# Adding the last expert blocks to the tokens by one-hot products instead of by scatter

## The chip, the cores and the metric

The kernel runs on one core of one Trainium2 chip. A core has engines that run side by side, each with its own instruction queue: TensorE (PE, matrix products; its weight loads are shown as PEld), VectorE (DVE), ScalarE (ACT), GpSimd (POOL) and SyncE (SP). They meet through semaphores. Sixteen DMA engines move data between the chip's DRAM and SBUF, the on-chip memory of 128 partitions; transfers are issued from the queues of SP, ACT and POOL. Products land in PSUM, from which DVE or ACT takes them. The metric is the device time of one execution in microseconds (us).

## The reference

Two layers over 625 tokens of width 768, with graph edges. Each layer adds a graph network and a linear attention to the tokens, and then a mixture of eight experts of which each token takes two:

```python
xn = _layernorm(x)
x = x + _L0_gnn_ref(xn, ...) + _L0_mix_ref(xn, ...)
x = x + _L0_ffn_ref(_layernorm(x), ...)     # 8 experts, top 2, three matrices each
xn = _layernorm(x)
x = x + _L1_gnn_ref(xn, ...) + _L1_mix_ref(xn, ...)   # graph attention
x = x + _L1_ffn_ref(_layernorm(x), ...)     # 8 experts, top 2, two matrices each
return x
# an expert mixture:
for e in range(8):
    h = gelu(x @ W1[e] + b1[e]); ...; y = h @ W_last[e] + b_last[e]
    out = out + gate[:, e:e+1] * y
```

All of it is f32. Biases and scales are random, so none of it can be left out.

## The kernel before

Tokens are kept in five blocks of T = 125. The experts work on gathered rows: a token's two places among its experts' rows are computed on chip (class Dispatch), and full blocks of 128 slots and half blocks of 64 slots are formed, each with one expert. Block numbers below NPB = 13 are full, those from 13 on half. RUN lists the 13 blocks that always run, in order; it ends in 8, 15, 9. MORE lists those which run only if the routing needs them; they stand in a conditional on the value `used` (L1330 in layer 0, L1681 in layer 1), which is not entered with these inputs.

A block gathers its token rows from DRAM by an indirect DMA on POOL (`gather`, L532), multiplies through the expert's matrices, scales by the gate into a tile `y` and adds `y` to the token rows of `sums_d[layer]`, in DRAM, by an indirect DMA with addition, again on POOL (`scatter_add`, L536). Two scatters into the same table go one after the other. `sums_d` was filled before with the tokens and the gated last biases. Layer 0's blocks are interleaved by hand (`blocks0`: six stages a block, a new block every three steps); a half block packs its two halves of columns into the two halves of the partitions, so its y has 128 rows of 384 and is added to half rows of the table. Layer 1's blocks (`block1`) load their weights on SP through shared buffers.

The order of instructions on each engine is found by a scheduler at build time, from the program's order and a model of times; dependencies are tracked by tile and region. In a conditional, nothing moves in or out.

Around layer 0's end: a tile `msum` with the counts of edges between tokens is loaded on ACT's queue (L1323), and behind the conditional 25 transposes (L1338) and 5 copies (L1339) make `mult` of it, used by the graph attention (`weights_of`, L1390 and L1410). Then layer 1 begins: for each token block, `sums_d[0]` is read (L367, on SP), normalised (L243 to L232), transposed (L187), multiplied by `L1_gnn_W1` (L201, 512 columns, 12 products of two instructions each) into `xl`, normalised again and transposed into `hT`. `sums_d[0]` is read once more much later, as the residual.

At the kernel's end, behind the second conditional, `sums_d[1]` is copied to the output in DRAM by two DMAs (L1683, L1685).

A few names: `ps_tile` gives one of four PSUM tiles of two banks; `token_rows` moves one block between DRAM and SBUF in two DMAs of 112 and 13 rows; `by_token` views a table as token blocks; `slabs` loads weights through five buffers of `wpool`.

Of the kernel before, what the change touches and what calls it, by code (L numbers as in the profile page):

```python
# [35 lines left out]
RUN = (0, 1, 2, 13, 3, 4, 5, 14, 6, 7, 8, 15, 9)  # L36
MORE = (10, 11, 12, 16, 17, 18, 19, 20)
# [6 lines left out]
def kernel(ctx: ExitStack, tc: tile.TileContext, a: dict, out: bass.AP):  # L44
# [83 lines left out]
    def blk(b):  # L128
        return slice(b * T, (b + 1) * T)
# [405 lines left out]
    def scatter_add(table_d, src, rows):  # L535
        nc.gpsimd.indirect_dma_start(out=table_d, out_offset=bass.IndirectOffsetOnAxis(ap=rows, axis=0),  # L536
                                     in_=src, in_offset=None, compute_op=OP.add)

# [651 lines left out]

    later = ctx.enter_context(ExitStack())
    multp = later.enter_context(tc.tile_pool(name="multp", bufs=1))
    mult = multp.tile([T, NB, N], F32, name="mult")


    with tc.tile_pool(name="msums", bufs=1) as msums:
        msum = msums.tile([128, NB, DQ * 128], F32, name="msum")
        with tc.tile_pool(name="work0", bufs=2) as moe:
            places_of = Dispatch(moe, moe, router)
            idx, es_i, used = places_of.idx, places_of.es_i, places_of.used  # L1200
            router.weigh()
            in_order.close()
            router.add_biases(x, moe)
            token_rows(by_token(sums_d[0]), x, True)
            es_hot, gate = places_of.gates()
            c1 = expert_biases(moe, moe, es_hot, columns_of["fb1"].rearrange("p (e c) -> p e c", e=8), 2, "c1")
            c2 = expert_biases(moe, moe, es_hot, columns_of["fb2"].rearrange("p (e c) -> p e c", e=8), 3, "c2")
            def hidden(a_, n, width, bias, name):

                ps = ps_tile()  # L1210
                for c in range(n):
                    nc.tensor.transpose(ps[:width, 0, c * 128 : (c + 1) * 128], a_[:, c * width : (c + 1) * width], ident)
                h_ = moe.tile([128, 3, 128], F32, name=name, bufs=3)
                for c in range(n):
                    nc.scalar.activation(h_[:width, c, :], ps[:width, 0, c * 128 : (c + 1) * 128], AF.Gelu,
                                         bias=bias[:, c : c + 1])
                return h_

            gates = []

            def block0(b, spare_pool=None):

                ex = nc.sync.value_load(es_i[0:1, b : b + 1], min_val=0, max_val=7)
                w12 = moe.tile([128, 1920], F32, name="w12", bufs=3)
                w1 = w12[:, :1152].rearrange("p (k o) -> p k o", k=KC)
                w2 = w12[:96, 1152:1920].rearrange("p (k o) -> p k o", k=2)
                nc.sync.dma_start(w1, expert(a["L0_ffn_W1"], ex).rearrange("(k p) o -> p k o", p=128))
                nc.sync.dma_start(w2, expert(a["L0_ffn_W2"], ex).rearrange("(k p) o -> p k o", p=96))
                w3 = (spare_pool.tile([128, 2304], F32, name="w3", bufs=1) if spare_pool else
                      wpool.tile([128, 2304], F32, name="w"))  # L1230
                w3 = w3.rearrange("p (k o) -> p k o", k=3)
                nc.sync.dma_start(w3, expert(a["L0_ffn_W3"], ex).rearrange("(k p) o -> p k o", p=128))
                if b >= NPB:
                    yield from block0_half(b, w1, w2, w3)
                    return
                xg = moe.tile([128, D], F32, name="xg", bufs=4)
                gather(xg, tokens_d[0], idx[:, b : b + 1])
                xT = moe.tile([128, KC, 128], F32, name="xT", bufs=3)
                evac(xT, to_slot_columns(xg, KC), b)
                yield  # L1240
                ps = ps_tile()
                for k in range(KC):
                    nc.tensor.matmul(ps[:, 0, :192], xT[:, k, :], w1[:, k, :], start=(k == 0), stop=(k == KC - 1))
                a1 = moe.tile([128, 192], F32, name="a1")
                nc.vector.tensor_copy(a1, ps[:, 0, :192])
                yield
                h1 = hidden(a1, 2, 96, c1[:, b, :], "h1")
                yield
                ps = ps_tile()
                for k in range(2):  # L1250
                    nc.tensor.matmul(ps[:, 0, :384], h1[:96, k, :], w2[:, k, :], start=(k == 0), stop=(k == 1))
                a2 = moe.tile([128, 384], F32, name="a2")
                nc.vector.tensor_copy(a2, ps[:, 0, :384])
                yield
                h2 = hidden(a2, 3, 128, c2[:, b, :], "h2")
                yield
                y = moe.tile([128, D], F32, name="y")
                ps = ps_tile()
                for h in range(2):
                    for k in range(3):  # L1260
                        nc.tensor.matmul(ps[:, h, :384], h2[:, k, :], w3[:, k, h * 384 : (h + 1) * 384],
                                         start=(k == 0), stop=(k == 2))
                if not gates:
                    gates.extend(gate())
                nc.vector.tensor_scalar(halves(y), ps[:, :, :384], gates[0][:, b : b + 1], None, op0=OP.mult)
                scatter_add(sums_d[0], y, idx[:, b : b + 1])

            def block0_half(b, w1, w2, w3):

                i = b - NPB  # L1270
                xg = moe.tile([128, D], F32, name="xg", bufs=4)[:64]
                gather(xg, tokens_d[0], idx[:64, b : b + 1])
                xT = moe.tile([128, KC, 128], F32, name="xT", bufs=3)[:, :, :64]
                evac(xT, half_slot_columns(xg), b)
                yield
                ps = ps_tile()
                for k in range(KC):
                    for j, p in enumerate(sides):
                        nc.tensor.matmul(ps[p, 0, :96], xT[:, k, :], w1[:, k, j * 96 : (j + 1) * 96],
                                         start=(k == 0), stop=(k == KC - 1))  # L1280
                a1 = moe.tile([128, 192], F32, name="a1")
                nc.vector.tensor_copy(a1[:, :96], ps[:, 0, :96])
                yield
                ps = ps_tile()
                nc.tensor.transpose(ps[:96, 0, :128], a1[:, :96], ident)
                h1 = moe.tile([128, 3, 128], F32, name="h1", bufs=3)
                for c in range(2):
                    nc.scalar.activation(h1[:96, c, :64], ps[:96, 0, c * 64 : (c + 1) * 64], AF.Gelu,
                                         bias=c1[:, b, c : c + 1])
                yield  # L1290
                ps = ps_tile()
                for k in range(2):
                    for p, c in zip(sides, (slice(0, 256), slice(256, 384))):
                        nc.tensor.matmul(ps[p, 0, : c.stop - c.start], h1[:96, k, :64], w2[:, k, c],
                                         start=(k == 0), stop=(k == 1))
                a2 = moe.tile([128, 384], F32, name="a2")
                nc.vector.tensor_copy(a2[:, :128], ps[:, 0, :128])
                nc.vector.tensor_copy(a2[:64, 128:256], ps[:64, 0, 128:256])
                yield
                ps = ps_tile()  # L1300
                nc.tensor.transpose(ps[:, 0, :128], a2[:, :128], ident)
                nc.tensor.transpose(ps[:, 0, 128:192], a2[:64, 128:256], ident[:64, :64])
                h2 = moe.tile([128, 3, 128], F32, name="h2", bufs=3)
                for c, at in ((0, 0), (2, 64), (1, 128)):
                    nc.scalar.activation(h2[:, c, :64], ps[:, 0, at : at + 64], AF.Gelu, bias=c2[:, b, c : c + 1])
                yield
                y = moe.tile([128, D], F32, name="y")[:, :384]
                ps = ps_tile()
                for k in range(3):
                    for j, p in enumerate(sides):  # L1310
                        nc.tensor.matmul(ps[p, 0, :384], h2[:, k, :64], w3[:, k, j * 384 : (j + 1) * 384],
                                         start=(k == 0), stop=(k == 2))
# [407 lines left out]
```

## Time and profile before

| what | us |
|---|---|
| median of three runs (2404.85 to 2409.11) | 2408.49 |
| the profiled execution's own time | 2404.86 |
| its span | 2403.1 |
| PE busy | 2227.3 (93%) |
| DVE busy | 932.2 (39%) |
| ACT busy | 278.0 (12%) |
| POOL busy | 467.1 (19%) |
| scatters L536: 26, mean | 1.58 each to issue |

Times in the profile count from the start of the span. Busy times are of the profiled execution alone. The slice rows cut the span into 40 equal parts, with each engine's busy tenths; a slice is 60 us, so what happens within 20 us needs the timeline, which lists instructions by start, duration, engine and line, like ones merged ("x12"), with the engine's idle time before them and what ended it. A DMA's row there is its issue, not its transfer. An engine's sequencer (PEq, SPq and so on) has rows for semaphores and branches, given by source line.

### The profile page before, as it was taken

The numbers are of one execution on the slowest core, as the hardware profiler recorded it, in microseconds if no ns is written. First come the engines' busy times: TensorE is split into PE (matmuls) and PEld (weight loads), VectorE is DVE, ScalarE is ACT, GpSimd is POOL, SyncE is SP. The second block draws the span as 40 slices with busy tenths as digits, with TensorE's granted clock in tenths as the row PEclk, the third lists the DMA queues.
The fourth block names the chain that finished last, engine by engine and source line by source line (L and its number), as shares of the span: only waits on it lengthen the run. The fifth ranks groups of instructions, "written<-read, shape, count | busy, mean of one in ns | idle before, by whom it ended". The sixth has DMA issues, their size and how long they took to land. (4 is left out here: it accounts for less than half of the span.)

```text
span 2403.1 us, 25088 instructions
## 1 busy us (share of the span) xinstructions
PE 2227.3 (93%) x10262; PEld 1473.7 (61%) x10262; DVE 932.2 (39%) x1930; ACT 278.0 (12%) x579; POOL 467.1 (19%) x261
## 2 busy tenths in 40 slices
PE   7999989999999999999999697799999998799996
PEld 4666556777776567777776454355776555455553
DVE  7554143444443333343352521623764534411110
ACT  2111000000001100000000122212552101011110
POOL 1676633232220022222210021000000200101100
PEclk9999999999999999999999799899999999799998
DMA  9435395444432051111101699112003200779785
GB/s 352 99 53 54 66 258 149 121 124 130 130 80 78 6 191 59 64 59 53 34 1 52 218 303 271 33 73 72 1 1 131 73 13 19 287 261 391 289 337 187
DMA packets 152834, 310.82 MB, mean 129 GB/s; under 512 B 49070, under 2 KB 70706, under 8 KB 152672
## 3 DMA queue, kind: packets, MB, share of 16 engines
q1 hardware_dynamic: 91154, 232.46, 27.6%
q0 software_dynamic: 52192, 49.28, 10.6%
q10 hardware_dynamic: 9358, 27.30, 3.4%
q8 instruction: 87, 1.43, 0.3%
q14 instruction: 43, 0.35, 0.0%
HBM read 249.09 MB, written 63.58 MB: 130 GB/s over the span
## 5 line engine op out<-in xcount | busy, mean ns | idle before, releaser
L912 PE MATMUL ps<-cnt,parts 125*128 125x314 bf16 x2880 | 392.3, 299 | 12.7 <-DVEq L1098 8.5
L912 PEld LDWEIGHTS <-parts 125*128 125x128 bf16 x2880 | 283.2, 98 | 121.4 <-issue 16.1
L668 POOL DMA_INDIRECT table<-val,idx x80 | 161.1, 2014 | 133.2 <-DMA table<-val,idx 58.6
L934 POOL TENSOR_TENSOR features<-w 128x1152 f32<-128x1152 f32 x14 | 37.3, 2666 | 521.7 <-issue 348.0
L960 PE MATMUL ps<-pair,w 128*128 128x314 f32 x504 | 136.8, 429 | 2.1 <-ACT pair L177 2.1
L1613 PE MATMUL ps<-w,xT 128*128 128x384 f32 x360 | 126.3, 502 | 11.3 <-DVE xT L175 6.7
L532 POOL DMA_INDIRECT xg<-tokens,d_idx x26 | 27.5, 1057 | 483.0 <-DVE gates L338 151.9
L960 PEld LDWEIGHTS ps<-pair,w 128*128 128x128 f32 x504 | 95.8, 190 | 40.4 <-ACT pair L177 2.6
L1626 PE MATMUL ps<-w,hT 128*128 128x384 f32 x360 | 119.2, 487 | 0.0
L201 PE MATMUL ps<-w,hT 128*125 128x384 f32 x360 | 117.8, 486 | 0.0
L1613 PEld LDWEIGHTS ps<-w,xT 128*128 128x128 f32 x360 | 68.0, 196 | 56.0 <-DVE xT L175 8.1
L177 ACT COPY features<-ps 128x628 f32<-128x628 f32 (+1 forms) x15 | 10.5, 703 | 766.2 <-PE ps L912 765.3
L201 PEld LDWEIGHTS ps<-w,hT 128*125 128x125 f32 x360 | 67.1, 188 | 46.9
L1626 PEld LDWEIGHTS ps<-w,hT 128*128 128x128 f32 x360 | 67.5, 190 | 45.0 <-issue 0.3
L1425 PE MATMUL ps<-xl,pT 125*125 125x256 f32 (+1 forms) x300 | 81.1, 427 | 12.4 <-ACT pT L177 8.8
L536 POOL DMA_INDIRECT sums<-y,d_idx x26 | 41.1, 1581 | 220.1 <-DVE y L1630 77.3
L881 PE MATMUL ps<-w,features 128*125 128x384 f32 x240 | 82.9, 504 | 0.0
L966 DVE TENSOR_TENSOR pair<-ps,pair 128x628 f32<-128x628 f32 (+1 forms) x60 | 44.8, 746 | 97.5 <-PE ps L960 97.5
L201 PE MATMUL ps<-w,features 128*125 128x384 f32 x240 | 80.0, 493 | 0.0
L1537 POOL TENSOR_TENSOR row<-row 128x768 f32<-128x768 f32 x1 | 1.8, 1813 | 395.9 <-DVE top L1395 395.9
L210 PE MATMUL ps<-features,w 128*128 128x313 f32 x288 | 77.4, 427 | 0.0
L1425 PEld LDWEIGHTS ps<-xl,pT 125*125 125x125 f32 x300 | 56.2, 191 | 34.1 <-ACT pT L177 10.3
(423 smaller groups left out, 3355.6 us busy)
## 6 DMA issues: line engine op xcount, KB each, us to landing
w<-in_L_ffn_w_dram SPq DMA_DIRECT2D x78, 1152.0 KB
w<-in_L_gnn_W_dram SPq DMA_DIRECT2D x34, 1152.0 KB
w<-in_L_ffn_W_dram SPq DMA_DIRECT2D x13, 1152.0 KB
table<-zero SPq DMA_DIRECT2D x32, 400.0 KB
cnt<-table POOLq DMA_DIRECT2D x16, 800.0 KB
edges<-cnt POOLq DMA_DIRECT2D x8, 1600.0 KB
w<-in_L_ffn_W_dram SPq DMA_DIRECT2D x13, 576.0 KB
w<-in_L_mix_W_qkv_dram SPq DMA_DIRECT2D x6, 1152.0 KB
```

Of the source, the lines that this page charges most:

```text
L201: nc.tensor.matmul(ps[:T, h, :width], xT[:, k, blk(b)], w_of(k)[:, h * width : (h + 1) * width], start=(k == 0), stop=(k == nk - 1))
L210: nc.tensor.matmul(ps[:width, h, :NH], w_of(k)[:, c0 : c0 + width], xT[:, k, h * NH : (h + 1) * NH], start=(k == 0), stop=(k == nk - 1))
L536: nc.gpsimd.indirect_dma_start(out=table_d, out_offset=bass.IndirectOffsetOnAxis(ap=rows, axis=0), in_=src, in_offset=None, compute_op=OP.add)
L668: scatter = nc.gpsimd.indirect_dma_start(out=table_of(g, j), out_offset=bass.IndirectOffsetOnAxis(ap=idx[:, j : j + 1], axis=0), in_=val[: ...
L881: nc.tensor.matmul(ps[:T, h, :384], aggs[:, k, blk(b)], w_of(k)[:, h * 384 : (h + 1) * 384], start=(k == 0), stop=(k == KC - 1))
L912: nc.tensor.matmul(ps[:, h, :HC], parts[:, b, i, k * 128 : (k + 1) * 128], cnt[:T, b, h * HC : (h + 1) * HC], start=(b == 0 and i == 0), s ...
L934: nc.gpsimd.tensor_add(wmix[:, 1], b11, b12)
L960: nc.tensor.matmul(ps[:, j, :HC], right[:, k, c : c + 128], left(k), start=(k == 0), stop=(k == K2 - 1))
L966: nc.vector.tensor_add(total, ps[:, :n, :HC], total)
L1425: nc.tensor.matmul(o, pT[:, j, :], xl[:, j, cols], start=(j == 0), stop=(j == NB - 1))
L1613: nc.tensor.matmul(ps[:, 0, :384], xT[:, k, :], w1_of(k)[:, q * 384 : (q + 1) * 384], start=(k == 0), stop=(k == KC - 1))
L1626: nc.tensor.matmul(ps[:, h, :384], hT[:, k, :], w2_of(k)[:, h * 384 : (h + 1) * 384], start=(k == 0), stop=(k == 8))
```

## The change

Blocks 15 and 9 (LAST) of layer 0, and block 9 of layer 1, are no longer scattered before the next stage. For each a 0/1 matrix `hot` (slots by 625 tokens) is made at dispatch, by comparing the slot's token number with a row of numbers. Once y is there, PE multiplies `hot` by y for each token block and half of the columns, and DVE adds the product to the token rows, which have been read back from `sums_d` without those blocks. A new class does it:

```diff
+    class Direct:
+        def __init__(self, pool, places, name):
...
+            nc.gpsimd.iota(self.number, pattern=[[1, N]], base=0, channel_multiplier=0, ...)
+        def slots(self, b):
...
+            nc.vector.tensor_scalar(self.hot[b], self.number, at, None, op0=OP.is_equal)
+            self.y[b] = self.pool.tile([128, D if b < NPB else 384], F32, name=f"{self.name}_y{b}", bufs=1)
+        def add(self, x, t, h):
+            ps = ps_tile()
+            out_ = ps[:T, h, :384]
+            bs = sorted(self.hot)
+            for b in bs:
+                p, c = (slice(0, 128), slice(h * 384, (h + 1) * 384)) if b < NPB else (slice(h * 64, (h + 1) * 64), slice(0, 384))
+                nc.tensor.matmul(out_, self.hot[b][p, blk(t)], self.y[b][p, c], start=(b == bs[0]), stop=(b == bs[-1]))
+            c = slice(h * 384, (h + 1) * 384)
+            nc.vector.tensor_add(x[:, t, c], out_, x[:, t, c])
```

In layer 0 the reads go on ACT's queue, six DMAs into the place of `xl` (now allocated before the experts), once before the conditional and once more at the end of its body. Behind the conditional stand the two scatters, for the later read of the sums, and the ten adds. `msum` is loaded only then, into the place of a later tile, and its transposes are done in layer 1's loop over token blocks, after the second transposes of each. The loop no longer reads DRAM. A full block of LAST scales its y in two halves.

```diff
-                    if step == 12 and spare_pool is None:
-                        nc.scalar.dma_start(msum, edges_d.rearrange("b p c -> p b c"))
...
+        def tokens_again():
+            for ts in ((0, 1), (1, 3), (3, NB)):
+                for p in (slice(0, 112), slice(112, T)):
+                    nc.scalar.dma_start(x1[p, ts[0] : ts[1], :], by_token(sums_d[0])[p, ts[0] : ts[1], :])
...
         blocks0(RUN)
+        tokens_again()
         w1_of = slabs(a["L1_gnn_W1"], 1024, 2)
         with tc.If(nc.values_load(used, min_val=0, max_val=2) > 0):
             blocks0(MORE, moe)
+            tokens_again()
+        for b in LAST:
+            if b < NPB:
+                scatter_add(sums_d[0], direct.y[b], idx[:, b : b + 1])
+            else:
+                scatter_add(half_rows(sums_d[0]), direct.y[b], places_of.idx2[:, b - NPB : b - NPB + 1])
         for b in range(NB):
-            ps = ps_tile()
-            sl = slots(ps, T)
-            for j in range(NB):
-                nc.tensor.transpose(sl[:, j, :], msum[:T, j, blk(b)], ident[:T, :T])
-            nc.scalar.copy(mult[:, b, :].rearrange("p (j c) -> p j c", c=T), sl)
+            for h in range(2):
+                direct.add(x1, b, h)
...
+        msum = lay.tile([128, 8 * NP], F32, name="gT")[:, : NB * DQ * 128].rearrange("p (b c) -> p b c", b=NB)
+        nc.scalar.dma_start(msum, edges_d.rearrange("b p c -> p b c"))
...
         for b in range(NB):
             xb = part.tile([T, 1, D], F32, name="part", bufs=3)
-            token_rows(by_token(sums_d[0])[:, b, :], xb[:, 0, :], False)
-            layernorm(xb, xb, D, [0])
+            layernorm(x1, xb, D, [b], [0])
             block_to_columns(xb, xnT, KC, b, 0)
...
+            multiplicities(b)
```

In layer 1 the sums are read on SP into `x` after the blocks of RUN, and the adds and the stores of the output follow before the conditional; its body repeats both. The copy from DRAM to DRAM is gone.

```diff
+            direct = Direct(keep, places_of, "end")
+            direct.slots(RUN[-1])
...
+            def tokens_again():
+                for b in range(NB):
+                    token_rows(by_token(sums_d[1])[:, b, :], x[:, b, :], False)
+            def finish():
+                for b in range(NB):
+                    for h in range(2):
+                        direct.add(x, b, h)
+                    token_rows(out[b * T : (b + 1) * T, :], x[:, b, :], True)
             blocks1(RUN)
+            tokens_again()
+            finish()
             with tc.If(nc.values_load(used, min_val=0, max_val=2) > 0):
                 blocks1(MORE)
-        nc.sync.dma_start(out[0:624, :].rearrange("(p r) d -> p (r d)", p=48), ...)
-        nc.sync.dma_start(out[624:N, :], sums_d[1][624:N, :])
+                tokens_again()
+                finish()
```

## The prediction

> **What bounds the kernel now.** The slice rows of the page come first: TensorE (PE) is busy in 93% of the span, and few slices fall below 9 tenths. The change touches two of them: the turn from layer 0's experts to layer 1 (about 1480 to 1515 us) and the last 20 us. The chain of waits ends with the last scatter (L536) and holds nothing of the copy to the output behind it, so I read the timeline. Columns: start, duration (us), engine, line, operation, in brackets the idle time before it.
>
> ```profile
> 2384.58 0.81 PE L1626 MATMUL ps<-w,hT 128*128 128x384 f32 x2
> 2385.43 1.02 DVE L1630 TENSOR_SCALAR y<-ps,d_gate 128x768 f32<-128x768 f32 x1 [11.38 <-PE ps L1626]
> 2386.72 1.55 POOL L536 DMA_INDIRECT sums<-y,d_idx  x1 [21.23 <-DVEq L1681]
> 2393.77 0.62 SPq L1683 DMA_DIRECT2D out_dram<-sums  x1
> 2394.76 0.50 SPq L1685 DMA_DIRECT2D out_dram<-sums  x1
> ```
>
> Nothing computes after 2386.5. The last 16.7 us are scatter (to 2392.7), then the 1.9 MB copy from DRAM to DRAM, issued at 2393.77; the rows of the kernel's last line have SP draining from 2402.2 and the end at 2403.1. The timeline of the turn:
>
> ```profile
> 1483.61 1.55 POOL L536 DMA_INDIRECT sums<-y,d_idx  x1 [7.65 <-issue]
> ...
> 1485.57 6.55 PE L1261 MATMUL ps<-w,h 128*128 128x384 f32 x12 [0.52 <-ACT h L1215]
> ...
> 1490.67 1.55 POOL L536 DMA_INDIRECT sums<-y,d_idx  x1 [5.51 <-DMA sums<-y,d_idx]
> ...
> 1494.17 2.96 PE L1338 MATMUL ps<-ident,msum 125*125 125x125 f32 x25 [2.05 <-DVEq L1330]
> ...
> 1496.50 1.57 POOL L536 DMA_INDIRECT sums<-y,d_idx  x1 [4.28 <-DMA sums<-y,d_idx]
> ...
> 1503.81 36.82 SPq L367 DMA_DIRECT2D part<-sums  x10
> ...
> 1507.57 1.02 DVE L243 BATCH_NORM_STATS2 ln_st<-part 125x6 f32<-125x384 f32 x2 [2.92 <-DMA part<-sums]
> ...
> 1513.50 12.67 PE L201 MATMUL ps<-w,x 128*125 128x512 f32 x24 [1.09 <-ACT x L177]
> ...
> 1528.64 10.56 PE L201 MATMUL ps<-w,x 128*125 128x512 f32 x24 [1.18 <-DVE x L175]
> ```
>
> The three scatters are those of blocks 8, 15 and 9. Each waits for the one before; the read of the sums waits for the third, and PE has no layer-1 matmul until 1513.50. The idle time is not empty: PE spends 2.96 us of it on the transposes of the edge counts, which nothing else needs yet.
>
> What the conditional costs is in the rows of its own line:
>
> ```profile
> L1330 SPq EVENT_SEMAPHORE  x9: 17/17/17, 1493.0 to 1500.0; - x9
> ```
>
> The branch isn't taken, but SP sits in it until its loads in flight have landed (7 us). An engine whose DMAs also occur in the untaken body waits so.
>
> **The end.** Removed: the last scatter and the copy, that is, everything after 2386.5. Added: 10 products (5 token blocks, 2 halves), 10 adds, 10 stores. A 128-row, 384-column f32 product is two instructions; 6 of them took 4.03 us (L1261 at 1459.01), 0.67 each. The scaling of y's first half (0.62, row of L1661) fits under the second half's matmuls, so the products start at 2385.5 and PE ends them at 2385.5 + 10 x 0.67 = 2392.2. An add is half of L359's 0.96 (768 wide), 0.5, so VectorE (DVE) keeps up with PE; its last one ends at 2392.9. The stores of blocks 0 to 3 go out meanwhile (375 KB per 1.34 us, 280 GB/s; the DMA rows show 348 to 422 at their best). The last store: the nearest row is the read of one block, issued 1503.81 and used at 1507.57, 3.76 us. So 2396.7. With 0.3 us for leaving the branch and the 1.0 us of closing that followed the last landing before, 2398.0: **5.1 us less**. The Trainium skill ("DMA: Bandwidth & Descriptors", Anatomy of one DMA) gives about 2.0 us fixed plus bytes over 436 GB/s: 2.9 us here, 6.3 for the copy that took some 8.3 in this trace. By it the end would come 0.9 us earlier; the page's figure is for another path and too low for the copy, so I take the row.
>
> The reads that this needs: 10 DMAs on SP, issued once block 15's scatter (2363.93) has landed. SP has nothing behind its weights (last issue 2357.8); the DMA engines are 1.03 to 1.07 busy until 2372 and at 0.02 from 2375 to 2386. 1.9 MB at 300 GB/s from 2373 ends at about 2380, hidden by 5 us; past 2386 each us would show in the end.
>
> **The turn.** Removed from the path: scatters 15 and 9, and the read behind them. Scatter 8 has landed by 1490.67. The six reads now go on the ACT queue (0.38 us an issue, row of L1323), with the weight load that SP issues at 1492.2 (1.15 MB) beside them: 3.07 MB at 348 GB/s are 8.8 us from 1492.3, 1501; with the reads served first, 1498. I take 1500. ACT can leave the branch only when all six have landed (the SP row above), so splitting them by block gives nothing. Queued behind this wait on ACT: the count load, the square roots, the copies of the transposed tokens.
>
> PE now has 20 products: 13.4 us. Four PSUM buffers let 8 of them run before 1500; the other 12 follow as DVE frees buffers, 8.1 us, so 1508.5; I say 1509 for part of it at half clock. If block 0's layernorm (3.3 us on DVE) slips between the adds, as the scheduler mixed L1372 of one block among L243 of the next, the transposes follow at 1509 and L201 some 2.3 us later: 1511.3 against 1513.50. It finds a warm PE: 10.56 instead of 12.67. Gain 2.2 + 2.1 = 4.3. For the warmth, the rule ("TensorE: Matmul & The Clock Gate", HAM clock gate) says that the clock halves after about 3.4 us idle and returns after as much work. The trace is harsher: granted clock 0.50 from 1484 to 1490 after gaps of 1.3 us. By the rule a PE that stood from 1496 to 1500 costs a further 2 us, by the row less idling is enough; this speaks against the change, and is why 1509 and not 1508.5, and its 2 us are in the range.
>
> Given back: the 25 transposes of the counts (2.96) now stand after each block's second transposes in a loop in which PE is busy for 11 to 12.5 of each 13.5 us. They go ahead of the next block's transposes, so they fill no gap, and their ACT copies (0.7) precede an ACT evacuation that PE awaits: 3.0 (0 if the scheduler puts them in the gaps of 1.1 to 2.3 us, 5 with the copies). The turn: -4.3 + 3.0 = **-1.3**.
>
> **Costed at nothing.** Block 15's scaling no longer waits 4.28 us for a y buffer; PE gains at least 0.6, but the reads end later anyway. The one-hots: two compares of 128x625 (0.48, row of L1390) and small casts, 1.5 us of DVE in 2.48 idle before L1245 at 1368; 0.7 in layer 1, in 3.17 idle before L1616 at 2075.8. Iota: POOL idles 145 us before its first gather. Count load (1600 KB) off 1339: the first expert matmul there follows L359, not data. Its new place is ACT's queue behind the reads: landed by about 1508, first needed at about 1522. The two late scatters, behind the branch on POOL, land by about 1515; POOL has nothing behind them until L1537, and the sums are next read at 1812.8. SP loses ten reads; its next load, at 1577, waits for a weight buffer, not for them. Uncovered, the one-hots cost 2.2.
>
> Sum: -5.1 - 1.3 = **-6.4** against the profiled execution (2404.86: span 2403.1 and 1.8 around it), about the lowest of the three runs. Off the median: 2408.49 - 6.4 = 2402.
>
> **Rivals.**
> (B) *The layernorm queues behind all ten adds on DVE.* For it: the adds are first in program order[...]. Against: the scheduler mixes lines elsewhere. Then the stats start at 1509.6 at best and L201 5.9 us later (1507.57 to 1513.50), 1515.5, on a cold PE; with reads at 1502 and the 12 products at half clock (1.28 each), 1524. Turn: 2.0 to 10.5 late, plus 3.0; total -0.1 to +8.4. It decides the sign from an L201 start of 1515.6 on. Time about 2413.
> (D) *The end gains nothing much*: reads later than 2386, or SP held in the last conditional. Against: 5 us of slack. 2407.
> (E) *Count transposes fall into gaps* and reads land at 1498: turn -6, total -11, 2397.5.
>
> **Chances.** Forecast 0.46, B 0.33, D 0.09, E 0.12. No change means within 0.2%, 4.8 us. Faster: 0.36 of the forecast's 0.46 (its own range is 2399 to 2405.5) and E, 0.48. Same: 0.10 from the forecast, 0.10 from B, 0.06 from D, 0.26. Slower: 0.23 from B, 0.03 from D, 0.26. The range of 2397 to 2416 leaves out the far ends of B and E.
>
> **What would show it.** Right: ten products after the last L1626 in about 6.7 us, a store issue near 2393 on the old clock and an end 5 us behind it; ACT leaving the first conditional near 1500; L201's first group 10.6 us long, starting near 1511. Wrong: block 0's stats after the tenth add (B); reads in the last conditional later than the last L1626 (D); more than 3 us between second transposes and the next L201 (a dearer loop).

## The result, and the profile after

The kernel got slower: 2419.26 us median (ten runs, 2411.55 to 2425.1) against 2403.73 (ten runs, 2400.08 to 2409.11), a ratio of 1.0059 with a 95% interval of 1.0048 to 1.0069. That is 15.5 us more, where the forecast was 6.4 less: it and its whole range of 2397 to 2416 were missed. The span of the profiled execution rose from 2403.1 to 2418.0.

Executions drift by some us before they reach the change, so I count from one instruction ahead of it that every kernel here has, the first product of layer 0's dispatch (L385 before, L386 after; at 1342.29 and 1339.88). From there to the first product of `L1_mix` (the row with `hT`), behind the turn and the loop over token blocks, before took 238.7 us and after 254.5: **15.8 lost in the turn and the loop**. The two rows, before and after:

```profile
1581.00 15.65 PE L201 MATMUL ps<-w,hT 128*125 128x384 f32 x48
1594.40 15.65 PE L202 MATMUL ps<-w,hT 128*125 128x384 f32 x48
```

From the last expert product to the end before took 17.7 (2385.39 to 2403.1) and after 14.9 (2403.14 to 2418.0): **2.8 gained at the end**. Another 4.3 us lie between the two: 1.1 up to layer 1's dispatch and 3.2 from there to the last expert product. Over the profiled executions below these two stretches ran from 467.6 to 472.1 us and from 336 to 340, in no order that goes with the edits, so I leave the 4.3 unexplained.

The timeline of the turn in the kernel after (start, duration, engine, line, operation; in brackets the idle time before it and what ended it):

```profile
1486.71 1.18 ACTq L1367 DMA_DIRECT2D xl<-sums  x3
1487.99 0.36 ACT L1252 ACTIVATE h<-ps,c 96x128 f32<-96x128 f32 x1 [14.03 <-DMA sums<-y,d_idx]
...
1488.40 2.93 PE L1291 MATMUL ps<-w,h 96*128 96x384 f32 x4 [9.87 <-ACT h L1252]
...
1500.74 16.81 PE L572 MATMUL ps<-last_y,last_hot 128*125 128x384 f32 x40 [1.78 <-DVEq L1380]
...
1503.09 0.56 DVE L244 BATCH_NORM_STATS2 ln_st<-xl 125x6 f32<-125x384 f32 x1
...
1518.35 0.68 DVE L233 TENSOR_SCALAR part<-xl,ln_mv,ln_r 125x768 f32<-125x768 f32 x1 [0.21 <-DVE xl L574]
...
1520.95 13.56 PE L202 MATMUL ps<-w,x 128*125 128x512 f32 x24 [0.88 <-ACT x L178]
...
1534.99 0.71 PE L1411 MATMUL ps<-ident,gT 125*125 125x125 f32 x5
...
1537.67 10.54 PE L202 MATMUL ps<-w,x 128*125 128x512 f32 x24 [1.33 <-ACT hT L194]
```

Read it from the top. L1367 is a read of the sums; L1252 is a gelu of block 9, the last expert block. The gelu stands *behind* three reads on ScalarE's queue, and ScalarE did nothing for 14 us. The rows of the read's own line say why:

```profile
L1367 ACTq DMA_DIRECT2D xl<-sums x6: 311/340/446, 1486.7 to 1493.4; - x6
L1367 ACTq EVENT_SEMAPHORE  x3: 17/17/13300, 1473.3 to 1487.1; - x3
```

The second row gives least, median and longest duration in ns: one semaphore wait of 13,300 ns, for block 8's scatter. TensorE, which needs that gelu, stood 9.87 us. Next, the 20 products took 16.81 us. Of their weight loads:

```profile
1503.22 0.29 PEld L572 LDWEIGHTS ps<-last_y,last_hot 64*125 64x125 f32 x2 [0.55 <-issue]
...
1504.06 0.29 PEld L572 LDWEIGHTS ps<-last_y,last_hot 128*125 128x125 f32 x2 [0.55 <-issue]
```

A product has two loads. Whenever the products change from 128 rows (block 9) to 64 (half of block 15) and back, the next pair of loads starts 0.55 us after the end of the pair before, 0.84 us from start to start. In the ten products at the kernel's end, which all have 128 rows, 18 loads take 5.57 us, 0.62 a pair. Block 0's statistics (L244, 1503.09) stand among the adds on VectorE, but its last step, the normalisation (L233, 1518.35), follows the tenth add, and the first L202 group is cold: it takes 13.56 us, not 10.56. In the windows (stretch, its length, busy time of PE, PEld, DVE, ACT, POOL, granted TensorE clock, DMA share, GB/s):

```profile
1510.00:1517.50 7.50, 7.50 (x19) 2.55 (x18) 2.23 (x4) 0.00 (x0) 0.00 (x0) 1.00 0.25 46
1517.00:1521.00 4.00, 1.43 (x9) 0.69 (x7) 3.17 (x7) 0.89 (x2) 0.00 (x0) 0.90 0.49 127
1521.00:1524.00 3.00, 3.00 (x4) 1.44 (x5) 2.65 (x14) 0.38 (x2) 0.00 (x0) 0.50 0.94 377
1524.00:1527.00 3.00, 3.00 (x4) 1.01 (x4) 2.93 (x15) 0.59 (x2) 0.00 (x0) 0.50 0.00 0
```

The clock was full from 1510 to the last product, and after two gaps of 1.69 and 0.88 us it was half for 6 us. The loop, from the first L202 to `L1_mix`, took 73.45 us against 67.5.

The end of the kernel after:

```profile
2403.17 1.14 DVE L1697 TENSOR_SCALAR end_y<-ps,d_gate 128x384 f32<-128x384 f32 x2 [11.38 <-PE ps L1691]
2403.84 6.71 PE L572 MATMUL ps<-end_y,end_hot 128*125 128x384 f32 x20 [0.71 <-DVE end_y L1697]
2404.37 5.57 PEld L572 LDWEIGHTS ps<-end_y,end_hot 128*125 128x125 f32 x18 [0.23 <-DVE end_y L1697]
2404.79 6.36 DVE L574 TENSOR_TENSOR x<-ps,x 125x384 f32<-125x384 f32 x10 [0.48 <-PE ps L572]
...
2406.02 6.74 SPq L366 DMA_DIRECT2D out_dram<-x  x10
```

Both halves of y are scaled only after the last expert product (2403.14); the ten products, all of one height, take 0.67 us each. The last add ends at 2411.15, the kernel 6.85 us later.

### The profile page after: what moved, and what is told of

Same layout as the page of the kernel before. It is cut to its first block, busy times and chain, and to the rows that moved or that the text cites. A ratio compares the mean times of both kernels' runs of the same rounds, so it can differ in the third digit from the quotient of the medians.

```text
span 2418.0 us, 25272 instructions
## 1 busy us (share of the span) xinstructions
PE 2251.4 (93%) x10322; PEld 1482.2 (61%) x10322; DVE 944.0 (39%) x1959; ACT 277.7 (11%) x579; POOL 468.3 (19%) x262
## 5 line engine op out<-in xcount | busy, mean ns | idle before, releaser
L949 PEld LDWEIGHTS <-parts 125*128 125x128 bf16 x2880 | 283.0, 98 | 122.1 <-issue 17.1
L202 PE MATMUL ps<-w,hT 128*125 128x384 f32 x360 | 117.8, 486 | 0.0
L202 PEld LDWEIGHTS ps<-w,hT 128*125 128x125 f32 x360 | 67.0, 188 | 47.0
L202 PE MATMUL ps<-w,features 128*125 128x384 f32 x240 | 79.6, 491 | 0.0
L997 PE MATMUL ps<-x,w 128*128 128x314 f32 x252 | 69.5, 435 | 4.1 <-DVE x L979 2.2
```

The source lines that it names most:

```text
L202: nc.tensor.matmul(ps[:T, h, :width], xT[:, k, blk(b)], w_of(k)[:, h * width : (h + 1) * width], start=(k == 0), stop=(k == nk - 1))
L949: nc.tensor.matmul(ps[:, h, :HC], parts[:, b, i, k * 128 : (k + 1) * 128], cnt[:T, b, h * HC : (h + 1) * HC], start=(b == 0 and i == 0), s ...
L997: nc.tensor.matmul(ps[:, j, :HC], right[:, k, c : c + 128], left(k), start=(k == 0), stop=(k == K2 - 1))
```

## The experiments

All times are compared with runs of the kernel before on the same chip; as the chips differ between groups of experiments, rows are best compared by their ratios. The third column counts from layer 0's dispatch to the first product of `L1_mix`, the fourth is the loop within it.

| kernel | ratio to before, 95% interval | to `L1_mix`, us | loop, us |
|---|---|---|---|
| before | 1 | 238.7 | 67.5 |
| after | 1.0059, 1.0048 to 1.0069 | 254.5 | 73.5 |
| e2: the end alone | 0.9996, 0.9983 to 1.0009 | 241.0 | 67.7 |
| e3: the turn alone | 1.0065, 1.0048 to 1.0081 | 255.4 | 72.2 |
| e1: reads behind the gelus | 1.0089, 1.0072 to 1.0107 | 260.7 | 74.1 |
| e5: e1, products in pairs | 1.0042, 1.0026 to 1.0058 | 249.6 | 73.0 |
| e6: e5, hot and y kept | 1.0052, 1.0036 to 1.0069 | 252.6 | 74.0 |
| e7: e6, products in the loop | 1.0196, 1.0176 to 1.0215 | 286.5 | 108.3 |
| e8: e6, counts early | 1.0053, 1.0036 to 1.0070 | 252.7 | 67.6 |
| e9: e7, counts early | 1.0216, 1.0196 to 1.0235 | 291.3 | 108.8 |
| e10: e6 without late scatters | 1.0018, 1.0005 to 1.0031 | 241.1 | 72.2 |
| e11: e6, slot numbers kept | 1.0008, 0.9994 to 1.0023 | 237.8 | 70.5 |
| e12: e8, slot numbers kept | 1.0019, 1.0006 to 1.0031 | 244.6 | 67.2 |
| e13: e11, counts in a gap | 0.9979, 0.9967 to 0.9991 | 235.6 | 65.7 |

Columns three and four are of one profiled execution each. e2 leaves the turn as it was and shows 241.0 there, so a difference of 2 us between two rows means nothing.

### Which half loses: e2 and e3

e2 takes layer 1's part of the diff alone, e3 layer 0's alone.

In code, e2 is layer 0 as before and layer 1 with `Direct(keep, places_of, "end")`, `tokens_again()` and `finish()`; e3 is layer 0 with `Direct(moe, places_of, "last")` and `tokens_again()`, and layer 1 and the output copy as before.

> The kernel before with the layer 1 part of the change alone (products, adds and stores at the end; layer 0 as before). The end of the changed kernel ran 14.9 us from the last expert product to the end of the span, against 17.7 before: 2.8 us. Theory Q: 2 to 3.5 us faster than the kernel before. Rival S (the layer 1 experts themselves get slower: they took some 2.7 us longer in the changed kernel's trace): no change, within 1 us.

> The changed kernel with the end of the kernel before (scatter, then the copy to the output); the layer 0 part alone. Theory Q: 15 to 18 us slower than the kernel before, all of it between 1478 and 1600 us. Rival S: about 12 us slower, with the rest of the loss in the layer 1 experts of the changed kernel.

e3 lost as much as the whole change (1.0065 against 1.0059). e2's trace ends 14.55 us after the last expert product, 3.1 less than before; the ratio of 0.9996 with its interval of about 3 us to either side neither shows nor excludes that gain. e3, which keeps the old end, took 16.75 us for it where before took 17.7, so the gain of the new end is some 2 to 3 us and rests on the traces alone. The loss is the turn's.

### The order on ScalarE: e1

`behind` is a helper of the kernel that holds an instruction in program order on its engine. In program order the reads stand after all of block 9.

```diff
-                    nc.scalar.dma_start(x1[p, ts[0] : ts[1], :], by_token(sums_d[0])[p, ts[0] : ts[1], :])
+                    behind(nc.scalar.dma_start(x1[p, ts[0] : ts[1], :], by_token(sums_d[0])[p, ts[0] : ts[1], :]))
```

> The changed kernel with one thing altered: the six reads of the sums stay behind block 9's gelus on ACT's queue. Theory Q (queue order): in the changed kernel ACT stood 14.0 us on a read that waits for block 8's scatter, with block 9's gelus behind it, and PE stood 9.9 us; with the order turned, PE's gap before block 9's second matrix falls to about 0.5 us, layer 1's first product (20.95 after 1500 in the changed kernel) comes 8 to 10 us sooner, and the time falls by about 9 us, to some 5 us above the kernel before. Rival R (the reads rule): the wait only shows the scatter's lateness; the reads land no sooner, so the products start hardly earlier and the time falls by less than 3 us.

The gap in block 9 went (L1291 now waits 0.51 us), but instead of the expected 9 us less the time rose further. Timeline, and windows of the products, of e1:

```profile
1481.14 1.56 PE L1291 MATMUL ps<-w,h 96*128 96x384 f32 x4 [0.51 <-ACT h L1252]
...
1484.42 4.14 PE L1301 MATMUL ps<-w,h 128*128 128x384 f32 x12 [0.52 <-ACT h L1252]
...
1488.41 2.84 ACTq L1367 DMA_DIRECT2D xl<-sums  x6
...
1493.08 31.48 PE L572 MATMUL ps<-last_y,last_hot 128*125 128x384 f32 x40 [4.53 <-ACTq L1380]
...
1528.62 12.49 PE L202 MATMUL ps<-w,x 128*125 128x512 f32 x24 [0.88 <-ACT x L178]
```

```profile
1493.00:1500.00 7.00, 6.92 (x9) 2.46 (x10) 1.64 (x3) 1.28 (x1) 0.00 (x0) 0.50 0.96 278
...
1510.00:1524.50 14.50, 14.50 (x19) 4.44 (x18) 2.23 (x4) 0.00 (x0) 0.00 (x0) 0.50 0.09 18
```

TensorE now waited 4.53 us ahead of the products, for ScalarE, which left the branch at 1493.0 with its reads issued. It began the products at half clock, and the clock stayed at 0.50 through 31 us in which the windows show TensorE busy: 1.57 us a product instead of 0.84. So the queue order is shown to be the cause of the 9.87 us; but the products, now behind a gap of 4.53 us, took 14.7 longer.

### Fewer changes of height: e5

e1, with both halves of block 9 multiplied before both halves of block 15, and one add 768 wide for both:

```diff
-            for h in range(2):
-                direct.add(x1, b, h)
+            direct.add_both(x1, b)
+        def add_both(self, x, t):
+            ps = ps_tile()
+            for b in sorted(self.hot):
+                for h in range(2):
...
+                    nc.tensor.matmul(ps[:T, h, :384], self.hot[b][p, blk(t)], self.y[b][p, c], ...)
+            nc.vector.tensor_add(halves(x[:, t, :]), ps[:T, :, :384], halves(x[:, t, :]))
```

> The first of these four (reads behind the gelus) with the layer 0 products of a token block in another order: both halves of block 9 (128 slots), then both of block 15 (64 slots), and one add of 768 columns instead of two of 384. In the changed kernel a product took 0.84 us where products of one height take 0.67 (at the end), and each change of height showed a weight load 0.55 us late. Theory H (each change of height costs about 0.17 us): half as many changes, so 20 products take 15 us instead of 16.8, and the time falls by 1 to 2 us against the first. Rival: the pace is set by DVE's adds or the four PSUM buffers; then the products take as long as before and nothing falls.

Windows of e5's products, and then its timeline:

```profile
1492.60:1496.00 3.40, 3.40 (x8) 1.44 (x8) 0.00 (x0) 1.28 (x1) 0.00 (x0) 0.56 1.05 317
1496.00:1500.00 4.00, 4.00 (x16) 1.63 (x12) 3.17 (x7) 0.30 (x1) 0.00 (x0) 0.94 0.83 222
1500.00:1506.00 6.00, 5.96 (x22) 2.22 (x20) 2.61 (x7) 0.00 (x0) 1.55 (x1) 1.00 0.27 33
```

```profile
1492.60 13.35 PE L583 MATMUL ps<-last_y,last_hot 128*125 128x384 f32 x40 [4.46 <-ACTq L1390]
...
1506.21 1.57 POOL L537 DMA_INDIRECT sums<-last_y,d_idx  x1 [3.47 <-issue]
...
1512.08 0.68 DVE L233 TENSOR_SCALAR part<-xl,ln_mv,ln_r 125x768 f32<-125x768 f32 x1 [5.12 <-DMA sums<-last_y,d_idx]
...
1512.96 1.48 PE L188 MATMUL ps<-ident,part 125*128 125x125 f32 x6 [7.01 <-DVE part L233]
```

Behind a gap of the same length (4.46 us) the same 40 instructions took 13.35 us, and half clock lasted some 3.4. The time fell by half a per cent against e1, more than the 1 to 2 us expected, since e1 had lost the clock. And a new wait came out: L233 writes `part`, and stood 5.12 us until the **late scatter** of `last_y` had landed. `part` lies where the experts' tiles lay, and the program does not reuse that memory while a scatter still reads from it. The transposes, and so the loop, waited for the writing of a result that nothing reads for another 300 us (the sums are next read at 1812.8 in the kernel before).

### Which memory: e6, e10, e11

e6 puts the one-hots and y of layer 0 into one tile of a pool that outlives the experts.

```diff
-        direct = Direct(moe, places_of, "last")
+        direct = Direct(moe, places_of, "last", arowp.tile([128, 4 * N], F32, name="arow"))
```

> The kernel with reads behind the gelus and products in pairs, and one thing more: the one-hots and y of blocks 15 and 9 lie in a tile that layer 1 takes only much later (the place of arow), instead of among the experts' tiles. In the run with pairs DVE's first normalisation stood 5.1 us until the late scatter of y had landed, and PE 7.0 us behind it. Theory W (reused memory): layer 1's tile has the place of y and must wait for the scatter; with y elsewhere PE's gap falls from 9.4 to about 2.5 us between the last product and layer 1's first matmul, and the time falls by 5 to 7 us against the run with pairs, to about 2409. Rival: the layernorm is late for another reason, and the time stays within 2 us of the run with pairs.

The wait of L233 on the scatter went, but the expected 5 to 7 us did not come (1.0052 against e5's 1.0042): the next wait in the row took its place. Timeline of e6:

```profile
1487.85 13.98 PE L592 MATMUL ps<-arow 128*125 128x384 f32 x40 [4.32 <-ACTq L1400]
1501.87 1.57 POOL L537 DMA_INDIRECT sums<-arow,d_idx  x1 [3.43 <-issue]
...
1508.21 0.39 ACTq L1423 DMA_DIRECT2D gT<-edges  x1
1508.63 1.28 ACT L218 ACT_TABLE_LOAD   x1 [28.77 <-issue]
...
1513.83 1.49 PE L188 MATMUL ps<-ident,part 125*128 125x125 f32 x6 [12.00 <-DVE part L233]
```

Now it is the count load, issued at 1508.21 on ScalarE's queue, with the square root of block 0's layernorm (L218) directly behind it. A scatter reads two things, its rows and the slot numbers by which it is addressed, `d_idx`; and `d_idx` was still in the experts' memory. e10 leaves the two late scatters out, and with them the rows of blocks 15 and 9 in layer 1's residual; e11 keeps them and gives the slot numbers a place of their own.

```diff
 e10:
-        for b in LAST:
-            if b < NPB:
-                scatter_add(sums_d[0], direct.y[b], idx[:, b : b + 1])
-            else:
-                scatter_add(half_rows(sums_d[0]), direct.y[b], places_of.idx2[:, b - NPB : b - NPB + 1])
 e11:
+    idxp = later.enter_context(tc.tile_pool(name="idxp", bufs=1))
-            self.idx = keep.tile([128, NS], I32, name="d_idx", bufs=1)
+            self.idx = (slots or keep).tile([128, NS], I32, name="d_idx", bufs=1)
...  (idx2 likewise)
```

> The kernel of e6_y_kept without the two scatters behind the conditional; it leaves the rows of blocks 15 and 9 out of the residual of layer 1, everything else is computed. Theory (what still holds the turn is memory that these two scatters read: ACT's count load, issued at 1508.2 when they have landed, with the square roots behind it): ACT issues the count load within 3 us of the branch (about 1491 to 1495), DVE's first normalise follows the adds at about 1502, and L202 of block 0 starts at about 1505 instead of 1516.2; the time falls by 9 to 11 us against e6, to a ratio of 0.9995 to 1.0015. Rival (the turn is bound by the products and the reads, not by the scatters): L202 within 2 us of 1516 and a ratio near 1.005.

> The kernel of e6_y_kept with the two tiles of slot numbers of layer 0 (idx, idx2) in memory that is not given to another tile; nothing is left out. Theory (of what the late scatters read, the slot numbers are what holds ACT's count load): as in the kernel without the late scatters, L202 of block 0 at about 1505, ratio 0.9995 to 1.0015. Rival (another tile of the experts' memory holds it, or the queue of POOL does): the count load is issued at about 1508 as before and the ratio stays near 1.005.

Timeline of e11, whose profiled execution runs some 13 us ahead of before's:

```profile
1480.31 14.37 PE L592 MATMUL ps<-arow 128*125 128x384 f32 x40 [4.69 <-PEq L1401]
...
1486.65 0.39 ACTq L1424 DMA_DIRECT2D gT<-edges  x1
...
1487.36 1.55 POOL L537 DMA_INDIRECT sums<-arow,d_idx  x1 [20.13 <-DVE ln_mv L245]
...
1490.66 0.68 DVE L233 TENSOR_SCALAR part<-xl,ln_mv,ln_r 125x768 f32<-125x768 f32 x1 [1.06 <-issue]
...
1494.61 0.86 PE L188 MATMUL ps<-ident,part 125*128 125x125 f32 x6
1496.35 10.56 PE L202 MATMUL ps<-w,x 128*125 128x512 f32 x24 [0.88 <-ACT x L178]
```

The count load goes out *before* the first late scatter has been issued, L233 runs during the products, the transposes follow the last product without a gap, and L202 takes 10.56 us: a warm start. From the dispatch L202 starts at 167.3 us, in e6 at 178.6, in before at 171.2. e10 and e11 agree within their intervals: what the late scatters cost was not their transfers or POOL's queue, but the memory from which they read. On the time this was worth 8 to 11 us (1.0052 to 1.0018 and 1.0008). e10's ratio is a little above the 1.0015 expected, and its count load was 6 us or more later than expected (issued at 1501.4; what holds it until then stays open); its L202 starts at 169.0.

One more thing goes with that memory: in e10 and e11 L233 stands among the adds, in after, e3, e1 and e5 behind the last one. The scheduler may have placed it there because of the scatter; no run tests that alone.

### The counts: e8, e12, and what failed: e7, e9

e8 is e6 with the counts loaded early again (into the place of `x`), transposed ahead of the conditional, and copied by VectorE; to make room, the experts' gathered rows have three buffers instead of four.

```diff
+                if step == 12 and spare_pool is None:
+                    nc.scalar.dma_start(msum, edges_d.rearrange("b p c -> p b c"))
...
         tokens_again()
+        for b in range(NB):
...
+                nc.tensor.transpose(sl[:, j, :], msum[:T, j, blk(b)], ident[:T, :T])
+            nc.vector.tensor_copy(mult[:, b, :].rearrange("p (j c) -> p j c", c=T), sl)
```

> As the kernel with y kept, but the edge counts are loaded early, as before the change, and their 25 transposes stand ahead of the conditional, where PE idles 4.5 us before the products (copies on DVE, three gather buffers instead of four to make room). Theory M: the loop gets back the 3.0 us of PE time that the moved transposes cost it, and the products meet a warm clock: 3 to 6 us less than with y kept. Rival: the transposes filled gaps in the loop anyway; less than 1.5 us.

The loop went back to 67.6 us from 74.0, but the time did not fall (1.0053 against 1.0052, where 3 to 6 us were expected): the products waited longer for the reads, and a compare of the counts (`far`) stood on VectorE, ahead of block 0's layernorm and the later adds, until a late scatter had landed. Timeline of e8:

```profile
1498.82 1.61 PE L592 MATMUL ps<-arow 128*125 128x384 f32 x2 [8.60 <-DMA xl<-sums]
...
1507.52 1.57 POOL L537 DMA_INDIRECT sums<-arow,d_idx  x1 [3.29 <-DMA sums<-arow,d_idx]
1513.82 0.49 DVE L1470 TENSOR_SCALAR far<-mult 125x625 f32<-125x625 f32 x1 [8.02 <-DMA sums<-arow,d_idx]
```

e12 is e8 with the slot numbers kept, the same edit as in e11.

> The kernel of e8_kept_early (counts transposed ahead of the conditional) with the slot numbers kept as well; nothing is left out. Theory: DVE's compare of the counts (`far`), which stood 8.0 us on a late scatter, no longer stands; the products still wait for the reads (8.6 us), so L202 of block 0 starts at about 1514 instead of 1522.9, the loop takes 67.6 us, and the ratio is 1.0015 to 1.0025. Rival (DVE's 8.0 us are hidden behind the products): L202 stays at 1521 to 1523, ratio 1.005.

The stand of `far` behind the scatter went, and L202 starts at 177.4 us from the dispatch instead of 185.1; the ratio of 1.0019 is the one expected. It stays behind e11. Its reads are issued 3.2 us after block 9's last product, e11's 3.8 us before its end, which fits a later start of the products; why block 8's scatter was late there stays open.

e7 moves e6's products into the loop over token blocks, to let the first block start after a fifth of them; e9 is e7 with the counts early as in e8.

```diff
-        for b in range(NB):
-            direct.add_both(x1, b)
...
             xb = part.tile([T, 1, D], F32, name="part", bufs=3)
+            direct0.add_both(x1, b)
             layernorm(x1, xb, D, [b], [0])
```

> As the kernel with y kept, but each token block's products and add stand in layer 1's loop, ahead of that block's layernorm. Theory L: layer 1's first matmul waits for 4 products instead of 20 and starts some 8 us sooner; the other 16 (10.7 us) partly fill PE's gaps of 1.2 to 2.4 us in the loop, so 2 to 6 us less than with y kept. Rival (PE is full in the loop): the 16 products only move, and the time is within 2 us of the kernel with y kept.

> Both of the last two together, all costs that I see taken out. If the theories hold, 2 to 6 us faster than the kernel before, the end's 3 us among it. If the products' PE time is what decides, still at or above the kernel before.

Both were expected to gain, and lost 30 us and more against e6 and e8, in the loop. Timeline of e7:

```profile
1525.80 2.30 PE L592 MATMUL ps<-arow 128*125 128x384 f32 x8
...
1533.88 1.48 PE L188 MATMUL ps<-ident,part 125*128 125x125 f32 x6 [5.78 <-DVE part L233]
```

Block 1's products follow block 0's L202 on TensorE, and its layernorm can begin only then: TensorE stands 5.5 to 5.8 us ahead of each of the other four blocks. In e6 the layernorm of the next block is done while L202 runs.

### The counts in a gap: e13

e11 with each block's count transposes one step earlier, where TensorE waits for the copy of the transposed tokens anyway.

```diff
             block_to_columns(xb, xnT, KC, b, 0)
+            multiplicities(b)
             evac(halves(xl[:, b, :]), token_matmul(xnT, w1_of, KC, b, 512), b)
...
-            multiplicities(b)
```

> The kernel of e11_slots_kept with each block's count transposes moved from behind its second transposes to behind its first ones, where TensorE waits 1.3 to 2.4 us for the copy of the transposed tokens; nothing is left out. Theory (the counts cost the loop 3 us because they stand where TensorE has no gap): the loop, first L202 to first product of L1_mix, takes 67 to 68 us instead of 70.5, no group of L202 starts at half clock, and the time falls by some 3 us to a ratio of 0.9990 to 1.0000, a small gain over the kernel before or none. Rival (the place makes no difference, since ACT's copies of the counts delay the copies that TensorE waits for, or the first block waits for the count load): the loop stays at 70 us or more, ratio 1.0008 or above.

Timeline of e13:

```profile
1513.60 0.78 PE L1431 MATMUL ps<-ident,gT 125*125 125x125 f32 x5 [1.13 <-DMA gT<-edges]
1515.17 10.56 PE L202 MATMUL ps<-w,x 128*125 128x512 f32 x24 [0.79 <-ACT x L178]
1525.57 1.45 PE L188 MATMUL ps<-ident,part 125*128 125x125 f32 x12
1526.85 0.71 PE L1431 MATMUL ps<-ident,gT 125*125 125x125 f32 x5
1528.44 10.54 PE L202 MATMUL ps<-w,x 128*125 128x512 f32 x24 [0.87 <-DVE x L176]
```

The gap ahead of the second L202 was 1.33 us in e11 and is 0.87 with the transposes in it; no group is cold, and the loop takes 65.7 us. The time is 2400.02 us against 2405.68, a ratio of 0.9979 (0.9967 to 0.9991): **faster than both kernels**, by 5 us against before and some 19 against after, and a little more than expected. The trace has 3.1 us less than before's in the turn and the loop, and 2.4 less at the end (last expert product 2392.1, span 2407.4). In the stretches between, where the only edit is layer 1's one-hot, this execution lost 6.9 us; it was the slowest of its twelve, so the 5 us rest on the twelve times and not on this trace.

## Why the prediction was wrong, point by point

The turn and the loop were forecast at 1.3 us less and took 15.8 more, a miss of 17.1. Of it, 12.1 lie ahead of the first L202 group (forecast 1511.3; on before's clock it started at 1523.4), and 5.0 in the loop.

**The step that failed first** is the order on ScalarE: "Queued behind this wait on ACT: the count load, the square roots, the copies of the transposed tokens." Block 9's gelus were missing from that list. The text said that the scheduler mixes lines, and used it for VectorE, but took program order for ScalarE. The scheduler had put three reads ahead of the gelus, and TensorE stood 9.87 us. e1 removes that gap, but loses the clock, so the gap's share of the time was never measured by itself. With the reads ahead of the gelus, the forecast's start of L201 could not come.

**The late scatters**, "POOL has nothing behind them until L1537", were costed at nothing because only their queue and the next reader of their result were asked about. What they hold is the memory that they read. In after no row waits for them: L233 comes behind the tenth add. e5 and e6 uncover the wait, and e10 and e11 show that it is worth 8 to 11 us once the first error is mended.

**The products**, "20 products: 13.4 us", were sized by a row of products of one height. With alternating heights they took 16.81 us at full clock and 31.48 at half (e1); in pairs 13.35, the first 3.4 of them at half clock. The ten at the end, all of 128 rows, took the 6.7 predicted.

**"It finds a warm PE: 10.56 instead of 12.67"** failed too: L202 took 13.56. Rival B had the late transposes, but not their cause. Its sign, block 0's statistics after the tenth add, did not show: they ran from 1503.09 on, among the adds, as the forecast had them, and only L233 came after the tenth. B's price stopped at +8.4 us because it had neither the queue nor the heights in it. In e11, where the layernorm runs among the adds as the forecast assumed, L202 takes the 10.56.

**The rule of the clock.** The Trainium skill ("TensorE: Matmul & The Clock Gate", HAM clock gate) would have left the clock full over gaps of 1.69 and 0.88 us; the trace has 0.50 behind them, as the row of before had shown. The other half of the rule, that the clock returns after about as much work, holds for e5 (half clock for some 3.4 us) and fails for e1 (not back in 31 us). The forecast set 0.5 us aside for half clock in the products, and 2 more in the range; in e1 it cost 14.7.

**The loop**, "3.0 (0 if the scheduler puts them in the gaps of 1.1 to 2.3 us, 5 with the copies)": after's loop lost 5.95, of which 1.7 are a cold fifth group (12.26) and 0.9 the colder first one (13.56 against 12.67); that leaves some 3.4 for the counts, so the size was right. The fifth group need not be the counts' doing: e12, with no counts in the loop, has a cold group of 12.26 too. e13 shows the 0 of the bracket.

**The end**, "5.1 us less": 2.8. "The scaling of y's first half ... fits under the second half's matmuls" was wrong: both scalings ran after the last product, which put the products 0.6 us later. The rest is the term of the stores: from the last add to the end 6.85 us against 3.76 + 0.3 + 1.0 = 5.1. One block's read, from before's trace, was too small a price for ten stores in a row and the branch behind them; how the 1.8 us divide between these two was not measured. The reads were hidden, as predicted, so rival D's mechanism didn't come.

**The conditional.** ScalarE left it at 1495.6, 1498.0 on before's clock and so near the forecast's 1500, but not for the reason given, "only when all six have landed". A window of after, with no other load issued between 1478.6 and 1499.0:

```profile
1496.00:1497.00 1.00, 1.00 (x4) 0.61 (x3) 0.00 (x0) 0.98 (x1) 0.00 (x0) 0.86 0.91 261
```

After ScalarE had left, 261 GB/s were still moving; from 1494 to 1498 it is some 0.8 MB, the size of the last two reads. So the time came out near by luck, and the products in after waited for y, not for the reads.

Right were the hidden reads at the end, the price of a product of one height, and the direction of each half once its waits were gone. e13 gains 5 us where the sum had 6.4, but that is made up otherwise: by the traces 3.1 in the turn and the loop against 1.3, and 2.4 at the end against 5.1. That the totals are close is partly luck.

## What to carry to other kernels

When a DMA is moved to a compute engine's queue, list what a scheduler may put *behind* it, compute of the stage before included: here the whole of ScalarE stood 14.0 us until the inputs of one read were there. A store or scatter that "nobody waits for" holds every tile that it reads, its addresses too (8 to 11 us here); before costing it at nothing, ask who gets that memory next. And price a chain of small products by one of the same shapes in the same order: 20 of them took 13.4, 16.8 or 31.5 us here.

## What the hardware showed that was not expected

A chain of f32 products of alternating height (128, 64 rows) that began at half clock stayed there for 31 us with no idle row in it (e1). The same chain behind a gap of 1.8 us kept the full clock (after, and e3 with the same 16.81 us). The same instructions with half as many changes of height regained it in some 3.4 us (e5), and in 5 to 6 us in e11 and e13, which use the pairs too. The profiled e1 is no odd one out: the clock granted over the whole execution is 0.963 to 0.968 in its six runs, against 0.968 to 0.972 in after's ten. In e1 each pair of weight loads at a change of height began 1.08 us after the end of the one before, in after, at full clock, 0.55. That TensorE counts these stretches as idle would explain it, but was only argued: e5 also halved the number of adds, and no run changed the heights alone.
